# Layer 3 of a four-layer kernel: six of sixteen scan inputs from TensorE instead of four, three of them in PSUM tiles lent by the exponentials

## The chip, the cores and the metric

The kernel runs on one core of a Trainium2 chip. The metric is the device time of one launch in microseconds. Three timed runs of the kernel before gave 24405.33, 24412.65 and 24425.22 us; the median is 24412.65 us. A separate profiled execution took 24438.58 us, and the span of its instructions, to which all times of the trace refer, is 24436.8 us.

## The reference, cut to what matters

Four layers follow one another on an input of 8 x 64 x 64 x 64 numbers in float32. The first is a spectral convolution, the other three contain state-space scans. The change touches the last, in which a bidirectional Mamba block runs once over one spatial axis and once over the other. Its core, for every channel `d` and each of 16 states `n`, is

```python
dA = jnp.exp(dt_t[:, :, None] * A)
h = h * dA + (dt_t * x_t)[:, :, None] * B_t[:, None, :]
y = jnp.einsum('bdn,bn->bd', h, C_t)
```

So for each state four things are made: the exponential `dA`, the product `du*B` with `du = dt*x` (the scan's input), the scan `h` itself, and the product `h*C`, which is summed over the states.

## The kernel before, in words

Layer 3 takes up the second half of the span. It walks over 256 steps: 2 axes x 16 chunks x 4 groups of 512 tokens x 2 directions `k`. A step holds 256 channels as a 128 x 1024 tile (two halves of 512 tokens side by side) and runs its 16 states one after the other. `stream` is a software pipeline over states: iteration `i` issues work of several neighbouring states, each engine gets its queue in exactly this order (the order is written by hand, nothing is rescheduled), and engines wait for each other through the tiles.

For state `n` of a step:

- `exponents` (L517): two ScalarE activations of 128 x 512 write `dA`. For ordinary states it lies in PSUM, in a ring of two tiles ("pe"); for the "direct" states it lies in SBUF, in a ring of four ("hb").
- `multiply_b` (L523): GpSimd multiplies `du` by `B` into a tile of the "hb" ring. For direct states (`fed`: 2, 6, 10, 14) this is left out. There, TensorE makes `du*B` with `expand` (L2182): eight matmuls of the transposed `du` (`duT`) against 128 x 128 matrices that hold `B` on their diagonal. The result goes to a PSUM tile "mm". There is only one tile "mm".
- The diagonal matrices come from memory: `place(e)` (L2103) scatters the 512 values of one state's `B` to the diagonal of a zeroed matrix in DRAM, and `load` fetches it (L2191) together with the broadcast `C` (L2192). For the other states one DMA fetches `B` and `C` (L2195). All of this is on the SP queue, six states ahead, into a ring of eight tiles "bc".
- `scan` (L545): VectorE scans over the 1024 columns. For states in `shared` the result goes to a tile of a ring of three ("h"), GpSimd multiplies it by `C` in place (`multiply_c`, L559), and TensorE adds it up three iterations after the scan. For the others VectorE multiplies too, into a ring of three ("hc").
- `gather`, `add_up` (L320): four 64 x 64 matmuls add `h*C` to the accumulator "acc". A tile of the ring "h" is free again when its gather has run.

Through the same tile "mm" goes everything that prepares the next step (`prepare`): the input projection (L2108), whose result ScalarE turns into `u`; the small projections L2123 and L2135, which ScalarE turns into `dbl` and `dt`; the gate L2152, turned into `z`; the transposes L2172, turned into `duT`. The table `plan` says at which state which pieces run, as (pieces ahead of the scan, pieces behind it). In between, every second step (those with `k` = 0), the output projection of the pair of steps just finished (`finish`: L2221 and L2224, copied out by L2240) takes "mm" at state 11; tasks that read the next chunk use it at 11 or 15 (`rooms`). `expand` of a direct state waits until all of these have given "mm" back.

The accumulator of a step is closed by VectorE after state 2 of the following step (L2202, "drain"); the same place in the order issues L2108.

## Time and profile before

| | us |
|---|---|
| median of three timed runs | 24412.65 |
| the profiled execution | 24438.58 |
| its span | 24436.8 |
| VectorE busy over the span | 21610.3 (88%) |
| GpSimd busy over the span | 21283.2 (87%) |
| TensorE matmuls busy over the span | 19876.3 (81%) |
| ScalarE busy over the span | 14851.8 (61%) |

Layer 3 is the stretch from about 11,300 us to the end, in which the slices look alike. The window from 14,000 to 24,000 us is used for its means: it holds 195.25 steps (781 scans of the four direct states), so a step takes 51.2 us there. In a row of the instruction groups the first number after the bar is busy time, the second the mean of one instruction in ns, the third the idle time of that engine just before these instructions, with what ended most of it. In the timeline the first two columns are start and duration in us, and brackets hold the idle time before the row.

### The profile page before, as it was taken

Reading aid. Unit: us, or ns where it says so; the run is one execution under the profiler, and the core shown is the slowest. Engines: PE = TensorE matmul, PEld = TensorE weight load, DVE = VectorE, ACT = ScalarE, POOL = GpSimd, SP = SyncE. Lnnn points to the kernel's source line nnn. Section 1 sums busy time; section 2 is a strip of 40 time slices with the busy share of each in tenths; the row PEclk is TensorE's granted clock in tenths of the full one; section 3 lists DMA queues with packets and bytes.
Section 4 is the critical chain, followed back from the end, with each engine's and each line's share of the span. In section 5 each row is a group of like instructions: output and inputs, shape, how many; then the busy total and the mean of one; then the engine's idle time right before and its main releaser. Section 6 shows DMA issues by size and latency. Waiting matters only on the chain. (4 is left out here: it accounts for less than half of the span.)

```text
span 24436.8 us, 270378 instructions
## 1 busy us (share of the span) xinstructions
PE 19876.3 (81%) x91034; PEld 8587.0 (35%) x91034; DVE 21610.3 (88%) x12457; ACT 14851.8 (61%) x19503; POOL 21283.2 (87%) x10196
## 2 busy tenths in 40 slices
PE   7778888888888888887777777777777777877777
PEld 5323333333333223323333333333333333333333
DVE  5599999999999689977999999999999999999998
ACT  5445555555555456624666667776666666666666
POOL 0499999999999579967999999999999999999998
PEclk9889999999999999998999999999988888888898
DMA  3699889889988579924555555555556555555555
GB/s 78 204 325 317 315 308 323 314 312 321 315 311 310 185 271 340 332 62 111 172 172 172 174 172 174 175 176 172 174 172 173 172 173 171 171 171 171 172 173 159
DMA packets 2518770, 5292.07 MB, mean 217 GB/s; under 512 B 1084760, under 2 KB 1091004, under 8 KB 2515072
## 3 DMA queue, kind: packets, MB, share of 16 engines
q1 hardware_dynamic: 2492800, 5211.44, 66.3%
q10 hardware_dynamic: 24576, 63.33, 0.7%
q8 instruction: 718, 11.76, 0.2%
q14 instruction: 676, 5.54, 0.1%
HBM read 5112.98 MB, written 160.31 MB: 216 GB/s over the span
## 5 line engine op out<-in xcount | busy, mean ns | idle before, releaser
L523 POOL TENSOR_TENSOR hb<-du,bc 128x1024 f32<-128x1024 f32 x3584 | 8392.3, 2361 | 809.2 <-DVE h L545 551.5
L545 DVE TENSOR_TENSOR_SCAN dA<-dA,hb 128x1024 f32<-128x1024 f32 x2680 | 6118.0, 2283 | 186.2 <-POOL hb L523 104.9
L523 POOL TENSOR_TENSOR hb<-du,b 128x1024 f32<-128x1024 f32 x2048 | 4879.4, 2414 | 464.2 <-DVE dA L545 196.5
L559 POOL TENSOR_TENSOR h<-h,bc 128x1024 f32<-128x1024 f32 x2016 | 4712.7, 2356 | 156.7 <-DVE h L545 156.3
L517 ACT ACTIVATE dA<-dt,w_A 128x512 f32<-128x512 f32 x6144 | 4184.8, 688 | 659.4 <-DVE hc L559 355.5
L517 ACT ACTIVATE dA<-dt,w_l_A 128x1024 f32<-128x1024 f32 x2560 | 2857.3, 1117 | 1004.8 <-DVE hc L559 765.1
L310 PE MATMUL acc<-hc,ident 128*128 128x512 f32 x7040 | 3377.6, 617 | 89.9 <-DVE img L1347 47.3
L559 DVE TENSOR_TENSOR hc<-dA,bc 128x1024 f32<-128x1024 f32 x2592 | 3174.4, 1225 | 173.4 <-issue 7.6
L545 DVE TENSOR_TENSOR_SCAN dA<-dA,carry,hb 128x1024 f32<-128x1024 f32 x1320 | 3094.5, 2344 | 122.7 <-POOL hb L523 60.4
L2182 PE MATMUL mm<-bc,duT 128*128 128x128 f32 x16384 | 2363.9, 304 | 772.4 <-ACT dt L435 348.0
L545 DVE TENSOR_TENSOR_SCAN h<-dA,hb 128x1024 f32<-128x1024 f32 x1032 | 2357.7, 2285 | 575.4 <-ACT dA L517 530.6
L2182 PEld LDWEIGHTS mm<-bc,duT 128*128 128x128 f32 x16384 | 2151.0, 212 | 1610.0 <-ACT dt L435 559.2
L545 DVE TENSOR_TENSOR_SCAN h<-hb,mm 128x1024 f32<-128x1024 f32 x1024 | 2322.5, 2268 | 326.6 <-PE mm L2182 170.5
L310 PE MATMUL acc<-h,ident 128*128 128x512 f32 x3200 | 1877.6, 717 | 881.8 <-POOL h L559 851.8
L320 PE MATMUL acc<-hc,ident 64*64 64x512 f32 x17920 | 2228.6, 599 | 0.1
L320 PE MATMUL acc<-h,ident 64*64 64x512 f32 x14848 | 2043.2, 659 | 134.8 <-POOL h L559 132.5
L310 PEld LDWEIGHTS acc<-hc,ident 128*128 128x128 f32 x7040 | 1392.7, 201 | 2084.3 <-issue 1712.0
L2108 PE MATMUL mm<-xn,taps 128*128 128x512 f32 x2048 | 1284.7, 785 | 729.0 <-DVE h L545 729.0
L559 DVE TENSOR_TENSOR hc<-dA,c 128x1024 f32<-128x1024 f32 x1408 | 1724.0, 1224 | 121.4 <-DMA c<-bc 7.8
L559 POOL TENSOR_TENSOR h<-h,c 128x1024 f32<-128x1024 f32 x640 | 1519.4, 2374 | 8.5 <-ACT carry L1330 8.0
L517 ACT ACT_TABLE_LOAD x1159 | 1487.0, 1283 | 20.6
L545 DVE TENSOR_TENSOR_SCAN h<-dA,carry,hb 128x1024 f32<-128x1024 f32 x600 | 1404.6, 2341 | 37.1 <-ACT dA L517 20.6
(333 smaller groups left out, 23128.6 us busy)
## 6 DMA issues: line engine op xcount, KB each, us to landing
bc<-bc SPq DMA_DIRECT2D x3072, 512.0 KB
b<-bc SPq DMA_DIRECT2D x2048, 512.0 KB
c<-bc SPq DMA_DIRECT2D x2048, 512.0 KB
bc<-bc SPq DMA_DIRECT2D x512, 1024.0 KB
bc<-dg SPq DMA_DIRECT2D x1024, 256.0 KB
bc<-bc SPq DMA_DIRECT2D x1024, 256.0 KB
tmp<-rs SPq DMA_DIRECT2D x93, 512.0 KB
raw<-x SPq DMA_DIRECT2D x256, 128.0 KB
```

The costliest lines, as they stand in the source:

```text
L310: self.nc.tensor.matmul(o, lhsT, r, start=start, stop=stop)
L320: self.nc.tensor.matmul(acc[j * C : j * C + C, r * 512 : r * 512 + 512], lhsT(j)[at, at], rhs[at, j * 512 : j * 512 + 512], start=start, s ...
L517: nc.scalar.activation(o[:, cut], s.dt[:, cut], AF.Exp, scale=A[:, n : n + 1])
L523: nc.gpsimd.tensor_tensor(s.shaped(hb[i]), s.shaped(s.du), B.pop(i), ALU.mult)
L545: nc.vector.tensor_tensor_scan(h[:, way], dA[i][:, way], b[:, way], s.first(n), ALU.mult, ALU.add)
L559: engine.tensor_tensor(s.shaped(o), s.shaped(h), CC.pop(i), ALU.mult)
L2108: nc.tensor.matmul(tokens(px[:, j * W : j * W + W]), w.taps[k][:, m, j * 128 : j * 128 + 128], xn[:, :, f : f + HW], start=m == 0, stop=m ...
L2182: nc.tensor.matmul(hb[:, at], self.duT[:, at], diag[:, m * 128 : m * 128 + 128], start=True, stop=True)
```

## The change

Direct states become 2, 5, 6, 9, 10, 13 (before: 2, 6, 10, 14). For 5, 9 and 13 (`lent`) the product `du*B` is written by TensorE into a tile of the exponentials' PSUM ring, since their own `dA` lies in SBUF. GpSimd no longer makes the input of 5, 9 and 13, and makes that of 14. State 13 is `shared` in all steps; before, it was so in one step out of four and VectorE multiplied it by `C` in the rest. The exponentials of direct states are issued one iteration earlier, ahead of ScalarE's copies out of "mm" in the next iteration. The transposes and `duT` move up by one state, there are six places a step in place of four, and the second room moves from 15 to 14. At state 13 a task that still holds "mm" is made to release it.

```diff
+        def lent(i):
+            return i % NS in steps[0].lent
...
         def expand(i):
-            if i < total and direct(i):
+            if i < total and direct(i) and lent(i):
+                hb[i] = steps[i // NS].expand(B.pop(i), pe.tile([128, T], F32, name="dA"))
+            elif i < total and direct(i):
                 while self.held:
                     self.release()
                 hb[i] = steps[i // NS].expand(B.pop(i))
...
-        expand(2)
+        if plan:
+            decay(2)
+            expand(2)
...
                 self.advance(behind, n in steps[0].rooms)
+                if n in steps[0].lets and self.held:
+                    self.release()
                 if i < total:
                     scan(i)
...
-                decay(i + 2)
-                expand(i + 3)
+                if not direct(i + 2):
+                    decay(i + 2)
+                elif lent(i + 2):
+                    expand(i + 2)
+                if direct(i + 3):
+                    decay(i + 3)
+                    if not lent(i + 3):
+                        expand(i + 3)
                 continue
...
-            fed = (2, 6, 10, 14)
+            fed = (2, 5, 6, 9, 10, 13)
...
-                direct, rooms = fed, (11, 15)
-                plan = {2: (0, 1), 3: (1, 0), 6: (0, 1), 7: (2, 0), 8: (1, 0), 9: (1, 0), 10: (0, 1), 11: (1, 0), 12: (1, 0), 14: (0, 1), 15: (1, 0)}
+                direct, lent, rooms, lets = fed, (5, 9, 13), (11, 14), (13,)
+                plan = {
+                    2: (0, 1), 3: (1, 0), 6: (0, 1), 7: (2, 0), 8: (1, 0), 9: (1, 0), 10: (0, 1), 11: (1, 0), 12: (1, 0), 13: (1, 1), 14: (1, 0)
+                }
...
-                    self.shared = (1, 2, 5, 6, 9, 10, 13, 14) if k and g % 2 else (1, 2, 5, 6, 9, 10, 14)
+                    self.shared = (1, 2, 5, 6, 9, 10, 13, 14)
...
                     place(3)
                     yield
+                    place(4)
+                    yield
                     px = pp.tile([128, T], F32, name="mm")
                     for m in range(T // 128):
                         at = slice(m * 128, m * 128 + 128)
                         nc.tensor.matmul(px[:, at], du[:, at], net.ident, start=True, stop=True)
                     yield True
+                    place(5)
                     self.duT = p1.tile([128, T], F32, name="duT")
                     nc.scalar.copy(self.duT, px)
 
-                def expand(self, diag):
-                    hb = pp.tile([128, T], F32, name="mm")
+                def expand(self, diag, hb=None):
+                    hb = pp.tile([128, T], F32, name="mm") if hb is None else hb
```

## The prediction

> **What bounds the kernel now.** First the busy shares of layer 3, from the table of stretches (stretch, length, then busy time and count of PE, PEld, DVE, ACT, POOL, granted clock, DMA share, GB/s).

> ```profile
> 14000.00:16000.00 2000.00, 1580.72 (x9564) 735.43 (x9556) 1862.55 (x1023) 1403.80 (x1911) 1881.36 (x820) 0.92 0.59 174
> ```

> VectorE and GpSimd are both 93 to 94% busy. Who waits for whom separates them, so next the instruction groups of 14,000 to 24,000 us (195.25 steps of 51.2 us).

> ```profile
> L523 POOL TENSOR_TENSOR hb<-du,bc 128x1024 f32<-128x1024 f32 x2343 | 5487.9, 2361 | 582.5 <-DVE h L545 413.4 <-DVE dA L545 89.0 <-DMA bc<-bc 67.1
> L559 DVE TENSOR_TENSOR hc<-dA,bc 128x1024 f32<-128x1024 f32 x1708 | 2092.0, 1225 | 112.7 <-issue 5.3 <-PE mm L2182 0.4
> L545 DVE TENSOR_TENSOR_SCAN h<-hb,mm 128x1024 f32<-128x1024 f32 x781 | 1771.4, 2268 | 245.0 <-PE mm L2182 114.5 <-PE acc L320 50.0 <-ACT dA L517 42.4
> L545 DVE TENSOR_TENSOR_SCAN h<-dA,hb 128x1024 f32<-128x1024 f32 x634 | 1449.3, 2286 | 428.9 <-ACT dA L517 399.0 <-POOL hb L523 19.7 <-POOL h L559 10.2
> ```

> GpSimd waits for VectorE; VectorE waits for ScalarE and TensorE. So VectorE sets the period: (428.9 + 245.0) / 195.25 = 3.45 us of idle a step, the remaining 47.75 us work with its hand-overs. Adding up the idle column of the timeline by state places it: 1.22 at state 5, 0.95 at 9, 0.21 at 10, 1.07 at 14 (means over all steps). State 5, read in the timeline:

> ```profile
> 18093.03 1.20 DVE L2202 TENSOR_TENSOR z<-acc,z 128x1024 f32<-128x1024 f32 x1
> 18093.17 5.43 PE L2108 MATMUL mm<-xn,taps 128*128 128x512 f32 x8 [3.83 <-DVE h L545]
> 18098.64 1.26 ACT L2119 ACTIVATE u<-mm,w_cb 128x512 f32<-128x512 f32 x2 [4.95 <-PE mm L2108]
> 18099.92 1.28 ACT L517 ACT_TABLE_LOAD   x1
> 18100.41 2.05 PE L2182 MATMUL mm<-bc,duT 128*128 128x128 f32 x16
> 18101.22 1.42 ACT L517 ACTIVATE dA<-dt,w_A 128x512 f32<-128x512 f32 x2
> 18102.39 1.95 PE L320 MATMUL acc<-h,ident 64*64 64x512 f32 x16
> 18102.73 2.29 DVE L545 TENSOR_TENSOR_SCAN h<-dA,hb 128x1024 f32<-128x1024 f32 x1 [1.57 <-ACT dA L517]
> ```

> Scan 5 waits for its exponential, behind a table load, `u`, and L2108. State 9 waits likewise behind `dt`. State 14 waits in every second step for the output projection that shares its tile "mm"; the chain that ended last shows this:

> ```profile
> 24357.87 1.97 PE mm L2221 x2
> 24359.84 5.77 PE mm L2224 x8
> 24365.61 0.02 issue
> 24365.64 0.69 ACT out L2240
> 24366.33 0.04 issue
> 24366.37 2.05 PE mm L2182 x16
> ```

> **Part 1, work removed from the two busy engines.** GpSimd loses the input products of 5, 9, 13, gains that of 14 and, in three steps of four, the `C` product of 13: (-3 + 1 + 0.75) x 2.36 = -2.95 us a step. Since it waits for VectorE, that earns nothing by itself. VectorE loses 0.75 multiplications of 1.225 us = 0.92 us. A larger value lies nearer: the period less its idle is 46.7 us in the steps that already share state 13 and 48.1 us in the others. I take 46.7 for all, so work falls from 47.75 by 1.05 us. Scans with `du*B` in PSUM take 2268 ns, those with `dA` there 2286: no difference that counts.

> **Part 2, state 5.** Time 0 is the drain (18093.03 above), D the duration of L2108. By the cadence above, scan 5 is due at +8.04. The exponential is now issued ahead of `u` and no longer late. Next late is the new `expand(5)`: in TensorE's order it stands behind L2108, the skip term and gather 0, that is 0.14 + D + 1.81 (the 18098.60 to 18100.41 above), and takes 2.05. Scan 5 can start at D + 4.05: idle D - 3.99, where the old chain gave D - 3.83. So almost nothing is gained. D is 3.7 when TensorE idled under 1 us before (44 steps), and in cold starts after idle 5.91 (3.3 to 3.6 us idle, 42 steps), 5.43 (3.6 to 4, 15 steps), 5.73 (4 to 4.5, 45 steps). How long will it idle then? Scan 10 ends at D + 20.6 (part 4). GpSimd then needs 1.0 more for the `C` product of 9, and seven products follow (input of 14, `C` of 10, inputs of 15, 0, 1, `C` of 13 and 14) at 2.33 us from one to the next: the last ends at D + 37.9, gathers 14 and 15 at D + 39.8. VectorE needs 22.7 us from the end of scan 10 to that of scan 2, so L2108 starts at D + 43.3 after 3.5 us of idle; in steps with an output projection (part 5) scan 13 and with it the input of 1 come later, and I count 4.6. So the two groups of steps with a warm start (mean D 3.70 and 3.86, two steps in eight) disappear. I take D = 5.7 everywhere, between 5.43 and 5.91: idle 1.71.

> **Part 3, state 6.** `expand(6)` follows at D + 3.93 and ends at D + 5.98; then gather 1, to D + 6.95. Scan 6 writes into the ring "h" of three, whose tile was state 1's, so it waits for that gather. It would be due 2.19 after scan 5, at D + 6.24, and starts at D + 7.0: idle 0.76, new. Before, this gather was done when scan 5 ended.

> **Part 4, states 9 and 10.** From scan 6: gathers 2 to 4 (0.89 each), L2123 (1.93), `dbl` (0.58), L2135 (1.13), `expand(9)` to D + 15.3, scan 9 due at D + 16.15. `expand(10)` and gather 5 end at D + 18.25, scan 10 is due at D + 18.33. Both idles go (1.16), with little to spare.

> **Part 5, states 13 and 14.** State 14 comes from GpSimd and needs no "mm": 1.07 goes. `expand(13)` needs only the tile of state 11, but stands on TensorE behind the output projection, in every second step. Queue: scan 9 ends at D + 18.41, then ScalarE runs the exponentials of 12 and 13, a table load, and `z` (1.42 + 1.3 + 1.28 + 1.02), so L2221 starts at D + 23.5. Behind it wait `expand(13)`, its scan, and all later gathers. L2221 and L2224 take 4.67 us warm (18071.25 to 18075.92) and 7.74 in the chain above. With 4.67, `expand(13)` ends at D + 30.2; scan 13 is due at D + 27.45, so idle 2.8; with 7.74 it is 5.9. Which? By the trace TensorE was busy 34% of the 3.4 us before the cold ones, and 59 to 67% before the warm. Here the gathers of 5 to 8 run right up to L2152, about 51%, nearer to the warm rows: 2.8, half of it per step, 1.4. Both ends stay for the range: cold ones follow gaps of only 1.1 to 1.4 us. In steps without an output projection `expand(13)` is in time.

> [...]

> **Part 6, the queues.** TensorE gains two expansions, 4.1 us a step. Its list then sums to some 41 of 50 us, so only the places above matter. ScalarE's count is unchanged. SP gains two places (0.62 each) and two `C` loads (0.43), 2.1 us. It spends 3552 us of the window waiting for GpSimd to free a "bc" tile, six states ahead, so I take nothing; uncovered it would be up to 2.1 us a step, below nothing it can't be. The first filling has four more DMAs of 0.26 MB: 6 us once at 174 GB/s, hidden behind the projections or not.

> **Sum.** Idle 1.71 + 0.76 + 1.4 = 3.87 against 3.45; work 46.7 against 47.75. Period 50.57 against 51.2, so -0.63 us x 256 steps = -161 us. The profiled execution (24438.58) would become 24278. It stands 26 us above the median of the runs, from which I subtract: 24412.65 - 161 = 24252 us.

> **Rivals.**
> - *Cold output projections (slower).* Three of four groups of them average 6.93 us. Then idle 13 is 2.8 + 2.26, +1.13 a step: 51.7, or +128 us, 24541. It decides from 5.93 us on (zero gain). For it: `z` waits longer than before, so the gap is 1.65 us instead of 1.13. Against: TensorE is fuller before.
> - *No measurable difference.* Warm and cold mixed near 5.9 us on average, 24413. A measurement can tell about 0.2% (49 us) from no change.
> - *Scan 6 isn't held.* If gather 1 gets in between, or the expansions overlap more than the 1.98 cadence: -0.76, 24057. Against: the order of the queue is fixed.
> - *L2108 warm.* The additional matmuls keep the clock up: D = 3.7, idle 5 zero, idle 6 0.45. That takes off another 2.02 a step: 23735. Against: the idle of 3.5 us before it is not shortened by the change.

> **Chances.** Forecast 0.40, scan 6 free 0.12, warm L2108 0.06: faster 0.58. No difference 0.15. Slower 0.27, nearly all of it cold projections, a little for SP. The range goes from the free scan 6 with some margin for D (0.2 us is 51 us) to the cold case with a D above 5.7: 24000 to 24580. It leaves out the warm L2108 and the tail of the slow side. The likeliest case alone, with D from 5.4 to 5.9, has 24175 to 24303.

> **What would show it.** Right: no idle at scans 9, 10, 14; about 1.7 at scan 5, now released by TensorE's expansion; 0.8 at scan 6, released by "acc"; 2.8 at scan 13 in every second step; GpSimd busy 2 to 3 us less a step; 50.6 us between drains. Wrong: L2108 at 3.7 us in most steps, output projections near 7 us, idle of VectorE behind GpSimd or a DMA, or a scan 10 that waits for gather 5.

## The result and the profile after

The changed kernel takes 24533.25 us (median of four runs, 24528.13 to 24536.05) against 24408.99 us before on the same chip: ratio 1.0053, 95% interval 1.0035 to 1.0070. It is 0.5% slower. A gain of 161 us was forecast, a loss of 124 us came. The profiled execution took 24534.96 us, its span 24533.2 us.

First the same stretch as before, from the table of stretches, with the same columns:

```profile
14000.00:16000.00 2000.00, 1662.97 (x10681) 848.50 (x10680) 1796.01 (x975) 1386.55 (x1879) 1741.70 (x757) 0.93 0.59 171
```

GpSimd and VectorE both became less busy, as the removed work says, and the time grew all the same. So the loss is idle time of both. The instruction groups of 14,000 to 24,000 us (194 steps) say where:

```profile
L526 POOL TENSOR_TENSOR hb<-du,bc 128x1024 f32<-128x1024 f32 x1937 | 4556.7, 2367 | 629.4 <-DVE h L550 267.7 <-DVE dA L550 202.8 <-DMA bc<-bc 150.6
L564 DVE TENSOR_TENSOR hc<-dA,bc 128x1024 f32<-128x1024 f32 x1549 | 1897.0, 1225 | 87.2 <-PE dA L2202 1.3
L550 DVE TENSOR_TENSOR_SCAN h<-hb,dA 128x1024 f32<-128x1024 f32 x582 | 1328.3, 2282 | 660.1 <-PE dA L2202 345.6 <-ACT hb L520 314.3
L550 DVE TENSOR_TENSOR_SCAN h<-hb,mm 128x1024 f32<-128x1024 f32 x581 | 1319.3, 2271 | 190.0 <-PE acc L320 178.9 <-ACT dA L520 11.1
L550 DVE TENSOR_TENSOR_SCAN h<-dA,hb 128x1024 f32<-128x1024 f32 x387 | 882.2, 2280 | 86.5 <-ACT dA L520 61.2 <-issue 20.5 <-PE acc L320 4.5
```

The third row is the new kind of scan, with the input in a lent PSUM tile: states 5, 9, 13. It alone has 660.1 us of idle ahead of it, 3.4 us a step, about as much as all scans together had before (345.6 us of it are scan 13, 314.3 us scan 5). Added up by state over all steps after 12,000 us (us per step):

| | period | 5 | 6 | 9 | 10 | 13 | 14 | 1 | 2 | sum |
|---|---|---|---|---|---|---|---|---|---|---|
| before | 51.25 | 1.22 | 0 | 0.96 | 0.21 | 0 | 1.07 | 0 | 0.02 | 3.48 |
| forecast | 50.57 | 1.71 | 0.76 | 0 | 0 | 1.40 | 0 | 0 | 0 | 3.87 |
| after | 51.66 | 1.64 | 0.54 | 0 | 0 | 1.83 | 0.30 | 0.14 | 0.41 | 4.86 |

Period less idle is 46.80 us after; 46.7 was forecast. The work fell nearly as counted, the idle rose by more than it.

Scan 5, whose idle the third row puts down to ScalarE's "hb":

```profile
15591.27 1.32 ACT L520 ACTIVATE hb<-dt,w_A 128x512 f32<-128x512 f32 x2
15599.89 2.05 PE L2202 MATMUL dA<-bc,duT 128*128 128x128 f32 x16
15600.70 1.33 ACT L520 ACTIVATE hb<-dt,w_A 128x512 f32<-128x512 f32 x2
15602.05 2.29 DVE L550 TENSOR_TENSOR_SCAN h<-hb,dA 128x1024 f32<-128x1024 f32 x1 [1.94 <-ACT hb L520]
```

The releaser named is not the real one. The exponential of state 5 is the first row, done 9.5 us before the scan; the third row is that of state 6, which scan 5 does not read and which happens to end as the scan begins. What was missing is `expand(5)`, the second row: it ends 0.11 us before the scan, the same distance as `expand(13)` and scan 13 below.

Scan 13 in steps with an output projection, first where TensorE kept its clock, then where it had lost it (mean granted clock over the projection 1.00 and 0.59); both from the timeline of the changed kernel (L2202 is `expand`, here for state 13):

```profile
15672.94 1.08 PE L2241 MATMUL mm<-raw,w_res 64*64 64x512 f32 x2 [1.72 <-ACT z L2178]
15673.95 3.65 PE L2244 MATMUL mm<-z,w_end 128*64 128x512 f32 x8
15677.53 2.05 PE L2202 MATMUL dA<-bc,duT 128*128 128x128 f32 x16
15679.69 2.29 DVE L550 TENSOR_TENSOR_SCAN h<-hb,dA 128x1024 f32<-128x1024 f32 x1 [2.70 <-PE dA L2202]
```

```profile
15566.44 1.97 PE L2241 MATMUL mm<-raw,w_res 64*64 64x512 f32 x2 [1.72 <-ACT z L2178]
15568.33 5.83 PE L2244 MATMUL mm<-z,w_end 128*64 128x512 f32 x8
15574.10 2.05 PE L2202 MATMUL dA<-bc,duT 128*128 128x128 f32 x16
15576.26 2.29 DVE L550 TENSOR_TENSOR_SCAN h<-hb,dA 128x1024 f32<-128x1024 f32 x1 [5.77 <-PE dA L2202]
```

The gap ahead of both is the same 1.72 us. One projection takes 4.66 us, the other 7.72; `expand(13)` and the scan behind it are later by just that. Of 102 projections from 14,000 us on 28 were slow (mean 7.78), all others took 4.66; before, 59 of 102 were slow. Warm means here a granted clock of 1.00 throughout, cold one that is 0.50 for a part of the time.

The trace's record of the granted clock shows what separates the two. In the traces of the kernel before and of the changed one it changes only at the ends of intervals of 3.41 us that follow one another on a fixed grid. Here are, for the slow projection and then for the other, the interval ahead of it and the one in which it starts (length, busy time and count of TensorE's matmuls, granted clock, DMA share, GB/s):

```profile
15562.53:15565.94 3.41, 1.57 (x9) 1.00 0.61 154
15565.95:15569.36 3.41, 2.92 (x4) 0.50 0.74 204
15668.35:15671.75 3.40, 2.62 (x20) 1.00 0.69 155
15671.76:15675.17 3.41, 2.23 (x5) 1.00 0.80 222
```

Where most of the idle time fell into one interval, which was then 46% busy, the next two had half the clock (0.50 from 15,565.95 to 15,572.77 us). Where it was split between two, 77% and 65% busy, the clock stayed at 1.00. The busy share of the 3.4 us directly ahead, wherever they lie on the grid, separates nothing: it was 42% ahead of nearly all projections, slow and fast. The share of the last whole interval was 45 to 48% ahead of 26 of the 28 slow ones and 50 to 84% ahead of the fast ones; the other two slow ones (6.36 us) began in an interval that was 52% busy, the fast ones in one of at least 58%.

Scan 14, in a step without a projection:

```profile
15416.43 1.23 DVE L564 TENSOR_TENSOR hc<-dA,bc 128x1024 f32<-128x1024 f32 x1
15417.73 1.28 ACT L520 ACT_TABLE_LOAD   x1 [4.07 <-DVE hc L564]
15419.03 2.75 ACT L520 ACTIVATE dA<-dt,w_A 128x512 f32<-128x512 f32 x4
15420.53 2.29 DVE L550 TENSOR_TENSOR_SCAN h<-dA,hb 128x1024 f32<-128x1024 f32 x1 [0.69 <-issue]
```

ScalarE idles 4.07 us with a table load to do, and begins it only when VectorE has given the exponential's PSUM tile free: this load waits with the exponential that needs it, for 790.1 us in the 194 steps of 14,000 to 24,000 us. The loads ahead of `z`, `u` and `dt` have only 3.4 us of idle each ahead of them there. Scan 14 then comes 0.69 us late.

Scan 2, in the one step of eight in which a task of the next chunk has the tile "mm" at state 14 (L2053 copies its mean out):

```profile
15688.99 1.32 ACT L520 ACTIVATE hb<-dt,w_A 128x512 f32<-128x512 f32 x2
15690.33 1.00 ACT L2053 COPY sq<-mm 1x1024 f32<-1x1024 f32 x1
15691.39 3.78 PE L2202 MATMUL mm<-bc,duT 128*128 128x128 f32 x16 [4.11 <-ACT sq L2053]
15695.10 2.19 PE L320 MATMUL acc<-h,ident 64*64 64x512 f32 x16
15696.61 2.29 DVE L550 TENSOR_TENSOR_SCAN h<-hb,mm 128x1024 f32<-128x1024 f32 x1 [3.29 <-PE acc L320]
```

The copy stands on ScalarE behind the exponentials of 1 and 2 (before, it stood behind that of 1 but ahead of that of 2); `expand(2)` waits for it and, after 4.11 us of idle, takes 3.78 us at a granted clock of 0.50 (`expand(13)` above took 2.05), the gather behind it comes late, and with it a tile of the ring "h".

Scan 1 waits in another step of eight, for another piece of such a task:

```profile
16462.69 1.08 ACT L2048 ACTIVATE sq<-raw 64x1024 f32<-64x1024 f32 x1 [2.95 <-DMA rs<-sq]
16463.68 1.39 ACT L520 ACTIVATE dA<-dt,w_A 128x512 f32<-128x512 f32 x2
16465.17 2.29 DVE L550 TENSOR_TENSOR_SCAN h<-dA,hb 128x1024 f32<-128x1024 f32 x1 [1.43 <-ACT dA L520]
```

The square of L2048 stands ahead of the exponential of 1 and waits 2.95 us for a DMA that still reads its tile "sq".

### The profile page after: what moved, and what is told of

It is laid out like the page before. It is cut to its first block, busy times and chain, and to the rows that moved or that the text cites. A ratio compares the mean times of both kernels' runs of the same rounds, so it can differ in the third digit from the quotient of the medians.

```text
span 24533.2 us, 289383 instructions
## 1 busy us (share of the span) xinstructions
PE 20446.8 (83%) x99226; PEld 9314.5 (38%) x99226; DVE 21394.5 (87%) x12265; ACT 14880.2 (61%) x19503; POOL 20542.7 (84%) x9876
## 5 line engine op out<-in xcount | busy, mean ns | idle before, releaser
L526 POOL TENSOR_TENSOR hb<-du,bc 128x1024 f32<-128x1024 f32 x3072 | 7218.7, 2365 | 899.7 <-DVE h L550 374.9
L564 POOL TENSOR_TENSOR h<-h,bc 128x1024 f32<-128x1024 f32 x2208 | 5196.5, 2365 | 787.7 <-DVE h L550 762.8
L550 DVE TENSOR_TENSOR_SCAN dA<-dA,hb 128x1024 f32<-128x1024 f32 x2488 | 5677.5, 2282 | 191.9 <-POOL hb L526 98.4
L520 ACT ACTIVATE dA<-dt,w_A 128x512 f32<-128x512 f32 x5120 | 3520.6, 689 | 1248.8 <-DVE h L550 660.2
L550 DVE TENSOR_TENSOR_SCAN h<-hb,dA 128x1024 f32<-128x1024 f32 x768 | 1752.7, 2282 | 878.3 <-PE dA L2202 461.5
L320 PE MATMUL acc<-h,ident 64*64 64x512 f32 x16384 | 2083.4, 614 | 254.9 <-POOL h L564 252.6
L2125 PE MATMUL mm<-xn,taps 128*128 128x512 f32 x2048 | 1437.7, 866 | 1017.1 <-DVE h L550 1017.1
L320 PE MATMUL acc<-hc,ident 64*64 64x512 f32 x16384 | 2047.2, 592 | 0.0
L520 ACT ACTIVATE hb<-dt,w_A 128x512 f32<-128x512 f32 x3072 | 2034.1, 709 | 6.1
L550 DVE TENSOR_TENSOR_SCAN h<-hb,mm 128x1024 f32<-128x1024 f32 x768 | 1743.8, 2271 | 245.2 <-PE acc L320 233.1
L2202 PE MATMUL dA<-bc,duT 128*128 128x128 f32 x12288 | 1637.8, 289 | 235.5 <-ACT dt L2182 228.3
L2202 PEld LDWEIGHTS dA<-bc,duT 128*128 128x128 f32 x12288 | 1491.7, 198 | 847.4 <-ACT dt L2182 306.8
L550 DVE TENSOR_TENSOR_SCAN h<-dA,hb 128x1024 f32<-128x1024 f32 x712 | 1622.9, 2279 | 137.3 <-ACT dA L520 102.2
```

The source lines that it names most:

```text
L320: self.nc.tensor.matmul(acc[j * C : j * C + C, r * 512 : r * 512 + 512], lhsT(j)[at, at], rhs[at, j * 512 : j * 512 + 512], start=start, s ...
L520: nc.scalar.activation(o[:, cut], s.dt[:, cut], AF.Exp, scale=A[:, n : n + 1])
L526: nc.gpsimd.tensor_tensor(s.shaped(hb[i]), s.shaped(s.du), B.pop(i), ALU.mult)
L550: nc.vector.tensor_tensor_scan(h[:, way], dA[i][:, way], b[:, way], s.first(n), ALU.mult, ALU.add)
L564: engine.tensor_tensor(s.shaped(o), s.shaped(h), CC.pop(i), ALU.mult)
L2125: nc.tensor.matmul(tokens(px[:, j * W : j * W + W]), w.taps[k][:, m, j * 128 : j * 128 + 128], xn[:, :, f : f + HW], start=m == 0, stop=m ...
```

## The experiments

**Theories.** A: the loss lies in the order of TensorE's and ScalarE's queues, in three places: the projection ahead of `expand(13)` with its clock, the table load, and the tasks of the next chunk. B: GpSimd, with the input of 14 and all products of 13, is the new limit. C: the added matmuls themselves are too much for TensorE.

All runs in one table: median, ratio to the kernel before on the same chip with its interval, then per step the period, the idle ahead of scans, and the slow projections (over 5.5 us) among those counted from 14,000 us on. Each is named by its edit. The kernels ran on several chips, on which the kernel before took 24399 to 24447 us, so small differences are better read from the ratios.

| kernel | us | ratio, 95% interval | period | 5 | 6 | 13 | 14 | 15, 0 | 1, 2 | drain | slow |
|---|---|---|---|---|---|---|---|---|---|---|---|
| changed | 24533 | 1.0053, 1.0035 to 1.0070 | 51.66 | 1.64 | 0.54 | 1.83 | 0.30 | 0 | 0.55 | 0 | 28/102 |
| room at 12 | 24533 | 1.0039, 1.0024 to 1.0053 | 51.69 | 1.80 | 0.54 | 0.08 | 0.59 | 1.23 | 0.54 | 0 | 0/102 |
| room at 12 only | 24675 | 1.0096, 1.0081 to 1.0111 | 52.19 | 2.58 | 0.57 | 0.06 | 0.61 | 1.29 | 0.17 | 0 | 0/102 |
| state 5 back | 24451 | 1.0006, 0.9997 to 1.0015 | 51.28 | 1.42 | 0 | 2.35 | 0.26 | 0 | 0.52 | 0 | 73/102 |
| zeros ahead of L2125 | 24317 | 0.9948, 0.9933 to 0.9963 | 50.68 | 0 | 0.25 | 2.49 | 0.20 | 0 | 0.43 | 0.53 | 85/101 |
| early table load | 24420 | 1.0008, 0.9998 to 1.0017 | 51.20 | 1.45 | 0.54 | 1.82 | 0 | 0 | 0.66 | 0 | 52/102 |
| zeros ahead of L2241 | 24412 | 1.0003, 0.9994 to 1.0013 | 51.20 | 1.63 | 0.54 | 1.39 | 0.30 | 0 | 0.54 | 0 | 0/102 |
| release at 14 | 24760 | 1.0146, 1.0130 to 1.0161 | 52.50 | 2.00 | 0.57 | 2.38 | 0.32 | 0.26 | 0.17 | 0 | 72/102 |
| table load and zeros | 24320 | 0.9960, 0.9945 to 0.9975 | 50.76 | 1.43 | 0.54 | 1.38 | 0 | 0 | 0.67 | 0 | 0/101 |
| the same and release | 24321 | 0.9960, 0.9946 to 0.9975 | 50.80 | 1.61 | 0.56 | 1.49 | 0 | 0.26 | 0.16 | 0 | 0/101 |
| reordered | 23894 | 0.9790, 0.9775 to 0.9805 | 49.10 | 0.59 | 0.45 | 0.05 | 0.62 | 0.04 | 0.58 | 0 | 0/101 |
| reordered, early table load | 23752 | 0.9732, 0.9716 to 0.9748 | 48.58 | 0.48 | 0.43 | 0.08 | 0 | 0.04 | 0.82 | 0 | 0/100 |
| the same, zeros ahead of L2125 | 23831 | 0.9764, 0.9750 to 0.9779 | 48.88 | 0 | 0.17 | 0.07 | 0 | 0.07 | 0.83 | 1.02 | 0/101 |

**Room at 12.**

```diff
-                direct, lent, rooms, lets = fed, (5, 9, 13), (11, 14), (13,)
+                direct, lent, rooms, lets = fed, (5, 9, 13), (12, 14), (13,)
```

> The output projection (and every task that takes the first room) runs at state 12 in place of 11, so it stands behind expand(13) in TensorE's queue. Theory A (the loss is TensorE's order): scan 13's idle, 1.83 us a step in the changed kernel, goes to about 0, the time falls by 1.83 x 256 = 470 us from 24533 to about 24065; GpSimd and the clock play no part. Theory B (GpSimd, with the input of 14 and all products of 13, is the new limit): the idle comes back at another scan, released by GpSimd, and the time stays within 100 us of 24533.

The idle at 13 went from 1.83 to 0.08, and the time stayed (within 35 us by the ratios). It came back at 15 and 0 (1.23) and at 14 (0.59), though not released by GpSimd, as B wants. The timeline of this kernel shows how:

```profile
12595.07 1.18 ACT L2260 ACTIVATE out<-mm,w_l_linb 64x512 f32<-64x512 f32 x1 [1.30 <-PE mm L2244]
12596.05 1.41 ACT L520 ACTIVATE dA<-dt,w_A 128x512 f32<-128x512 f32 x2
12597.54 2.30 DVE L550 TENSOR_TENSOR_SCAN dA<-dA,hb 128x1024 f32<-128x1024 f32 x1 [1.40 <-ACT dA L520]
```

ScalarE waits with the projection's copy out, which the release at 13 puts ahead of the exponential of 15. So the cause of 13 was right and the sum wrong: a wait moved from TensorE's queue into ScalarE's.

**Room at 12 only.** `rooms` is `(12,)`.

> As the kernel with the room at 12, and the second room (14) is gone, so that the tasks that read the next chunk use only state 12. Theory A2 (the idle at scans 1 and 2, 0.14 + 0.41 us a step, comes from such a task that keeps the tile mm at state 14, ahead of expand(2)): both go, about 140 us less than with the rooms 12 and 14, near 23925. Rival: these idles come from GpSimd's late product of 13 or from a late DMA, and stay; then the two kernels are equal within 50 us.

The idle at 2 went (0.39 to 0), that at 1 stayed. But with one room the tasks of the next chunk end too late: L2125 waited 233.9 us in the window for their `xn`, which shows as 2.58 at scan 5. This miss tells nothing against A. It shows that the second room was needed, and that the idle at 1 has another cause than the copy.

**State 5 back.** `fed` is `(2, 6, 9, 10, 13)`, `lent` is `(9, 13)`, and the last `place` is gone.

> State 5 gets its input from GpSimd again (and its exponential in PSUM, behind u); all else as changed. Theory A (expand(5) earns nothing, it only replaces ScalarE as the releaser of scan 5 and delays scan 6): idle 5 stays 1.5 to 1.9, idle 6 (0.54) goes, GpSimd gains 2.36 us a step without being late: 24533 - 138 = about 24395. Theory B (GpSimd limits): 2.36 us more a step on GpSimd shows, the time rises by 100 to 600 us.

Idle 5 stayed a wait of its old kind (1.42), idle 6 went, and 2.36 us more of GpSimd a step cost nothing: B falls. The time fell by 82 us (about 115 by the ratios) instead of 138, since 73 of 102 projections were now slow (13: 2.35).

**Zeros ahead of L2125** (16 zero-weight matmuls behind the last gather):

```diff
+            if last and plan:
+                rhs = hc.get(i + 1, steps[at].u)
+                for j in range(4):
+                    steps[at].nothing(acc[at], rhs, j == 3)
```

> Four zero-weight 64 x 64 matmul groups (16 matmuls) are added to the accumulator behind the last gather of a step, waiting for the product of state 0, so that TensorE isn't idle ahead of the input projection; the sum is unchanged. Theory A (the input projection's 5.4 to 6.6 us are a clock that has fallen during 3 to 6 us of idle): it takes 3.7 us in nearly every step, idle 5 (1.64) goes to 0, idle 6 to about 0.3, 1.9 x 256 = 480 us less, about 24050. Rival (the matmuls are slow for another reason, such as their operands or the reading engines): it stays above 5 us and the time is the same or longer by the added matmuls.

The input projection took 3.74 us (mean 5.63 in the changed kernel), in all steps but one of 241 under 4.2, and idle 5 went to 0. In the trace of the changed kernel it took 3.77 us in the 29 steps in which the granted clock stayed at 1.00, and 5.17 to 6.72 us in the other 212, with 2.98 to 6.11 us of it at 0.50. So its length goes with the clock, and C falls: 16 matmuls more made the kernel faster. Half the expected gain was lost, mostly to slower output projections (13: 2.49) and a drain that waits for the added matmuls (0.53).

**Early table load.**

```diff
                     nc.scalar.copy(dt.rearrange("p (s t) -> p s t", t=HW)[:, :, at], endless)
+                    nc.scalar.activation(early, net.eps5, AF.Exp)
```

> The changed kernel with one 128 x 1 exponential more on ScalarE, right behind the copy that follows z, so that the table load doesn't wait with the exponential of state 14 for the product of state 12. Theory A (scan 14's 0.67 us in steps without an output projection, 0.30 in the mean, is that load): idle 14 goes to 0, 0.30 x 256 = 77 us less, about 24455. Rival (the exponential itself is late, 1.42 us behind the product of 12): 14 stays and the time is the same within 30 us.

Idle 14 went to 0 and 113 us with it (77 expected; idle 5 fell by 0.19 too). More projections were slow, 52 of 102, but these took 6.36 us, like the two of the changed kernel that had half the clock for one interval of 3.41 us and not two, so idle 13 stayed at 1.82.

**Zeros ahead of L2241.**

```diff
+                if n == steps[0].rooms[0] and self.urgent and not self.held and i < total:
+                    for _ in range(2):
+                        steps[at].nothing(acc[at], steps[at].u, False)
                 self.advance(behind, n in steps[0].rooms)
```

> The changed kernel with two groups of zero-weight matmuls (8 matmuls, some 1.8 us) ahead of each output projection, in the 1.72 us in which TensorE waits for z; the sum is unchanged. Theory A (the projections of 7.7 us are a fallen clock, and scan 13's 5.8 us in one step of eight is its price): all projections take 4.7 us, idle 13 goes from 1.83 to 1.4, 0.4 x 256 = 110 us less, about 24420. Rival (those projections wait for their operands or the clock doesn't follow the load): the projections stay as they are, the time is the same or up to 30 us longer.

Every projection took 4.66 us (598 ns for a matmul with `w_end`, 679 in the changed kernel), idle 13 fell to 1.39, the time by 121 us. Together with the pair of timelines and the intervals above this ties the slow projections to TensorE's idle time ahead of them.

**The kernel before, with zeros ahead of L2108.**

> The kernel before with four groups of zero-weight matmuls behind the last gather of each step, as in the changed kernel with them. Theory A (half of the idle that the change meant to remove is the clock of the input projection): L2108 takes 3.7 us, idle 5 goes from 1.22 to about 0, up to 1.2 x 256 = 310 us less, about 24100. Rival (the projections turn cold instead, as in the changed kernel with the added matmuls, or the drain waits for them): idle 14 and the drain take back half or more, gain below 150 us.

It took 24270.89 us, ratio 0.9945, 95% interval 0.9931 to 0.9960. Idle 5 went to 0 and the drain took back 0.87 a step; 14 fell only to 0.92. The gain was 128 us against the expected 310, below the rival's 150, though by the drain: the output projections were no colder than before (53 of 102 slow).

**Reordered.** The projection runs at 12; its copy out, the transposes and `duT` go back by one state; the second room is 15, released at once.

```diff
-                direct, lent, rooms, lets = fed, (5, 9, 13), (11, 14), (13,)
+                direct, lent, rooms, lets = fed, (5, 9, 13), (12, 15), (14, 15)
-                    ... 13: (1, 1), 14: (1, 0)
+                    ... 13: (1, 0), 14: (0, 1), 15: (1, 0)
```

> The output projection at state 12, behind expand(13), as in the kernel with the room at 12; but its copy out, the transposes and duT go back by one state (released at 14, transposes behind scan 14, duT at 15), and the second room goes to 15 with a release at once. Theory A (in the kernel with the room at 12 the idle came back at 14, 15 and 0 because ScalarE's copy out stood ahead of the exponentials of 15 and 0, and at 2 because the mean's copy stood behind the exponentials of 1 and 2): idle at 13, 15, 0 and 2 goes to about 0, 1.7 at 5, 0.55 at 6 and 0.6 at 14 stay: 46.8 + 2.9 = 49.7 us a step, 2.0 less than changed, about 24030. Rival (TensorE is simply too long in this stretch, whatever the order): the idle turns up at scan 1 or 2, released by expand(2) or a gather, and the time stays above 24350.

23894.15 us, faster than expected: the idle at 13, 15 and 0 is gone, and TensorE now idles less ahead of the input projection (2.4 us in the median, 4.45 in the changed kernel), and this starts warm in two steps of three (mean 4.43 us, 5.63 there), which the expectation left out. What each of the moves gave by itself was not run.

**Release at 14.** `lets` is `(13, 14)`.

> The changed kernel with one edit: a task that takes mm at state 14 (the mean of the next chunk) is released at once, so that its copy stands on ScalarE ahead of the exponentials of 1 and 2. Theory A (scan 2's 3.3 us in one step of eight is that copy): idle 2 goes from 0.41 to 0, 0.41 x 256 = 105 us less, about 24425. Rival (gather 13 or a DMA is late by itself): idle 2 stays, the time is the same within 30 us.

This was a miss: idle 2 went as expected, and the kernel became 227 us slower. 72 of 102 projections were slow, and the step that had started warm behind the late task now started cold (L2125 took 920 ns a matmul in the mean, 863 in the changed kernel). These groups of 14,000 to 24,000 us show it, the first row with 825.3 us of idle ahead of the lent scans (660.1 in the changed kernel), the second with 806 ns for a matmul of the projection (679 there).

```profile
L550 DVE TENSOR_TENSOR_SCAN h<-hb,dA 128x1024 f32<-128x1024 f32 x572 | 1305.4, 2282 | 825.3 <-PE dA L2202 446.9 <-ACT hb L520 378.5
L2244 PE MATMUL mm<-z,w_end 128*64 128x512 f32 x760 | 490.2, 806 | 0.0
```

**Table load and zeros ahead of L2241 together, without and with the release at 14.**

> The changed kernel with the early table load and the two groups of zero-weight matmuls ahead of each output projection: two of the terms that the prediction missed, taken out together. Theory A (the forecast was right but for the idle that the runs showed at 14, at 13 by cold projections, and at 1 and 2 by the next chunk's tasks): idle 14 goes to 0 and 13 to 1.4; 0.30 + 0.43 = 0.73 us a step, 187 us less than 24533, about 24345, faster than before by 0.3%; what is left to 24252 is the idle at 1 and 2. Rival (the parts interact, such as an input projection that starts colder): above 24400.

> As the kernel with the table load and the zero-weight matmuls, and the task at state 14 released at once, the third missed term. With the projections kept warm the release can't be hidden by colder ones, as it was when it was done alone. Theory A: idle 2 (0.41) goes, scan 0 takes 0.26 back, and in one step of eight the input projection loses its warm start (0.2): 24300 to 24345, within 50 us of the kernel without the release. Rival (the release costs by itself, by ScalarE's wait ahead of the exponentials): more than 80 us slower than without it.

The first took 24319.67 us: two terms out, and the change is faster than before by 0.4% (0.9945 to 0.9975). The second took 24320.90: with the projections kept warm the release costs nothing, and gains nothing, as scan 0, scan 13 in one step of eight (the mean's matmuls, 1.0) and the lost warm start take back what scan 2 gives. So the 227 us came through the clock, whose mean was 0.920 with the release alone, 0.928 in the changed kernel, and 0.933 and 0.935 in these two.

**Reordered with the early table load, and with zeros too.**

> The reordered kernel (projection at 12, transposes behind 14, release at 14 and 15) with the early table load. Idle 14 (0.62) goes, 0.62 x 256 = 160 us less: about 23735. Rival: GpSimd, whose input of 14 follows at once, takes over; then the gain is below 60 us.

> The reordered kernel with the early table load and three groups of zero-weight matmuls behind the last gather. Idle 14 (0.62), 5 (0.59) and part of 6 (0.45) go; the drain may wait some 0.3 for the added matmuls: 0.62 + 0.59 + 0.2 - 0.3 = 1.1 us a step, 284 us less than the reordered kernel, about 23610. Rival (the input projection starts later behind the added matmuls and the drain waits, as in the kernels with four groups): no faster than with the table load alone, 23735 or more.

23752.06 us, 2.7% faster than the kernel before, is the best version; the lent scans (5, 9, 13) now wait 0.5 us a step, in the same window:

```profile
L550 DVE TENSOR_TENSOR_SCAN h<-hb,dA 128x1024 f32<-128x1024 f32 x603 | 1374.3, 2279 | 108.9 <-ACT hb L520 91.0 <-PE dA L2204 15.9
```

The added zeros were a miss there: where most steps start warm already, the drain's wait for them (1.02) is more than they save.

## Why the prediction was wrong

- **Part 1 (work):** right, but for 0.1 us: 46.80 us of work a step, 46.7 forecast; GpSimd isn't the limit.
- **Parts 2 to 4 (states 5, 6, 9, 10):** right. 1.64 and 0.54 for 1.71 and 0.76, nothing at 9 and 10. `expand(5)` did take the place of ScalarE as the late one, in projection and other steps alike (the row's "ACT hb" is the exponential of state 6), and the warm groups of steps did nearly disappear (one step in eight was left, behind the late task).
- **Part 5, state 13:** the step that failed first. The two prices were right: 2.70 warm (2.8 forecast), 5.8 cold (5.9). The choice between them was not: I took all projections as warm from a busy share of 51% over the last 3.4 us. That share was 42%, and it doesn't decide: one of four groups of steps was cold at the same share and the same gap as the others, and already before the change 5 of 43 warm projections had 33 to 34%, as the cold ones had, and the same gap of 1.13 us. What separated them in the trace was how the idle time fell on the intervals of 3.41 us: the last whole one was 45 to 48% busy ahead of 26 of the 28 cold ones, 50 to 84% ahead of the warm. The term cost 0.43 us a step more, 121 us by the run that kept all projections warm.
- **Part 5, state 14:** it was said to go without a wait. The table load ahead of its exponential, behind `z`, does not stand in the reckoning; in fact it waits with the exponential for the product of state 12 (4.07 us in the rows above): 0.30 us a step, 77 us; the run with the early load gained 113 us, idle 5 included.
- **Parts 5 and 6, tasks of the next chunk:** left out: 0.55 us a step at scans 1 and 2. At 2 (0.41) the exponential of 2 went ahead of the copy that frees the tile; with the release at 14 this idle went, but nothing was gained in the sum. At 1 (0.14) the square that waits for a DMA is the cause by the timeline; no run took it away. In the reordered kernel 0.58 is left, mostly at 1.
- These three are 0.43 + 0.30 + 0.55 = 1.28 us, less 0.29 at 5 and 6: 0.99 x 256 = 253 us, of the 285 us between forecast and result. The 0.10 us of work a step that Part 1 counted too little are another 26 us; the last 6 us are well below what the medians of the kernel before differ by from chip to chip.

The rival with cold projections named 24541 us and the result is 24533, but for its reason only in part: it had three of four groups cold, there was one. The agreement of the two numbers is chance.

## What to carry to other kernels

Moving a product to an engine with spare time puts it into that engine's queue: ask what stands directly ahead of it, and move that behind it (here one state) together with everything whose wait would follow it onto the next queue, for a single edit only shifted the idle from scan 13 to scans 15 and 0. A table load can wait with the instruction that needs it, as the one ahead of scan 14's exponential did for 4.07 us: where the trace shows this, give it a small instruction of its own where the engine idles (idle 14 went from 0.30 to 0 by that). Where a matmul group has two lengths in the trace (here 4.66 and 7.72 us, at a mean granted clock of 1.00 and 0.59), don't choose one from a mean busy share: put both into the forecast with the shares that the trace shows, and read the granted clock by its intervals. The slow share can move with edits elsewhere: it was 28 of 102 in the changed kernel, and 73 with state 5 back on GpSimd.
